# Mask pieces made between the steps of the first graph, and a last group of steps by halves of its queries, in a masked attention layer over eight graphs

## The chip, the cores and the metric

The kernel runs on one core of a Trainium2 chip. The metric is the device time of one execution in microseconds, lower being better. The kernel before takes 3193.34 us, the median of three runs (3188.96 to 3195.69).

## The reference

Eight graphs of 2048 nodes with 256 channels share one adjacency matrix of int32 zeros and ones (2048x2048), which is the attention mask. All values are f32.

```python
qkv = x @ w_qkv                                  # x: (8, 2048, 256)
q, k, v = split(qkv), each as 8 heads of 32
scores = einsum('fnhd,fmhd->fhnm', q, k) / sqrt(32)
attn = softmax(where(adj > 0, scores, -1e9))
t = einsum('fhnm,fmhd->fnhd', attn, v)           # back to (8, 2048, 256)
y = layernorm(x + t) * ln1_g + ln1_b
h = relu(y @ w1 + b1)
z = layernorm(y + h @ w2 + b2) * ln2_g + ln2_b
out = layernorm(x + z)                           # mean and variance over the 256 channels
```

## The kernel before

The work is cut into 1024 items (L543): graph `f`, chunk `qc` of 512 queries, half `g` of the heads (four heads), block `mb` of 128 keys, the last fastest. One graph is 128 steps (`FRAME`), one group (f, qc, g) is 16. Step t of the loop at L606 does, in this order on each engine's queue: `advance(t)`, which issues side work; the exponentials of item t+1 on ScalarE (ACT, L237); the scores of item t+2 on TensorE (PE, L230), each half of them followed by an addition of the mask on VectorE (DVE, L233) from PSUM into a `p` tile; the values of item t on PE (L249); and `add_up` (L264), which sums the exponentials for the softmax denominator. Of 16 items, six are added on GpSimd (POOL, L271) into the first, six go by accumulating DMAs of POOL's queue (L268) into two more chain heads. The three chain heads and item 15 are then reduced by matmuls with a constant (L315) in `denominator` (L297). Scores use three pairs of PSUM banks; two more banks alternate between the values' sums and side work, so side work has one bank a step.

The engines run in program order each, and the program writes that order out. The order of the side work is set by a small planner, `advance` (L511). Side jobs are generators in a list sorted by due step. A job yields `BANK` when it needs the side bank, `MORE` when it goes on in the bank that it has, `WAIT` when it must hold it, or a number of steps to sleep. Each step grants a credit of 2200 (`STEP`), at most 2200 (`KEPT`); a transposition of four blocks costs 1400, a unit of four matmuls of 512 columns 2048, and a job starts while 1024 are left or when it is due. Side jobs of a plain graph are the transposition of the next graph's x (`turn`: an SP load of x at L172, five steps later the transposes at L95 and copies at L166, then a write to DRAM), its queries (`ask`), its keys and values (`project`), started by the table `NEXT` (L553), and, for each query chunk, `denominator`, `outcome`, `divide` and `tail` (L297 to L377): division by the denominator (L356), first norm, feed-forward, second and third norm. A norm (L274) takes statistics on DVE (L278, L279), four small operations on POOL (L283 to L287) and scales on ACT (L290).

The mask is kept as 8-bit pieces of 128 keys x 2 blocks x 512 queries. `begin` (L557) makes all of them ahead of the loop, from 16 chunks of the adjacency matrix of 512 queries x 512 keys, in the order of query chunk: each chunk is loaded by SP (1 MB), turned to bf16 on DVE (L582), transposed on PE (L141), brought to 8 bits by ACT (L147) and DVE (L145) in turn, and written to a DRAM table `MD` (L148). After the last chunk of `qc` 1 `begin` issues the scores of items 0 and 1 and the exponential of item 0 (L598); the chunks of `qc` 2 and 3 follow, and then the loop starts. In the loop `load_mask` (L150) reads the pieces back for the next query chunk, one every other step of the groups with g = 1.

At the end, the last chunk's closing is `finish` (L443): after the last step it divides all 512 queries, and then runs two halves of 256 rows through norm, feed-forward and norms by turns (`half_rows`, L396). The chunk before it goes through `tail` with x already loaded (`xb`) and two statistics a step.

Of the kernel before, what the change touches and what calls it, by code (L numbers as in the profile page):

```python
# [10 lines left out]
F32 = mybir.dt.float32  # L11
# [50 lines left out]
def fast_path(ctx, tc, cst, x, adj, out, RS):  # L62
# [61 lines left out]
    MD = dp.tile([NCK, MB // 2, P, 2 * CH // 4], I32, name="md")  # L124
    MK = {}

# [7 lines left out]
    def mask_blocks(qc, mc, cv, to=None):  # L134
        for half in range(2):
# [12 lines left out]
            nc.sync.dma_start(MD[qc, k], words(m))  # L148

    def load_mask(f, qc, k):  # L150
        nc.sync.dma_start(words(mask_piece(f, qc, k)), MD[qc, k])
# [17 lines left out]
    def turn(f, c):  # L169
        yield INPUTS - 2  # L170
        xc, xT = take([P, TPC, C], F32), take([P, 2, CH], F32)
        nc.sync.dma_start(xc, x[f, c * CH:(c + 1) * CH, :].rearrange("(j p) c -> p j c", p=P))  # L172
        yield 5
        yield from turn_rows(xc, xT)
        give(xc)
        yield 1
        nc.sync.dma_start(XD[f][c], xT)
        XT[f, c] = xT
        give(xT)
# [38 lines left out]


    PT, O, OT, RC, DT = {}, {}, {}, {}, {}  # L220

    def scores(item):
        f, qc, g, mb = item
        pt = PT[item] = pp.tile([P, 4, CH], F32, name="p")
        ps2 = [score_pair() for _ in range(2)]

        for half in (1, 0):
            for j in range(2):
                r = D * (2 * half + j)
                nc.tensor.matmul(ps2[half][:, j, :], KT[f, mb // TPC, g][r:r + D, (mb % TPC) * P:(mb % TPC + 1) * P],  # L230
                                 QT[f, qc, g][r:r + D, :], start=True, stop=True)
        for half, ps in enumerate(ps2):
            nc.vector.tensor_tensor(pt[:, 2 * half:2 * half + 2, :], ps,  # L233
                                    MK[f, qc, mb // 2][:, mb % 2, None, :].to_broadcast([P, 2, CH]), ALU.add)

# [5 lines left out]
    def values(item):  # L241
        f, qc, g, mb = item
        grp = (f, qc, g)
        if mb == 0:
            i = state["side"]
            O[grp] = ps_x[i].tile([P, CH], F32, name=f"x{i}")
        for h in range(4):
            r = D * h
            nc.tensor.matmul(O[grp][r:r + D, :], V[f, mb // TPC, g][:, mb % TPC, r:r + D], PT[item][:, h, :],  # L249
                             start=(mb == 0), stop=(mb == LAST))  # L250
        if mb == LAST:
            OT[grp] = op.tile([P, CH], F32, name=f"oT{g}")
            nc.scalar.copy(OT[grp], O.pop(grp))
# [6 lines left out]

    ENDED = MB - 5
    SUM = 4

    def add_up(item):  # L264
        f, qc, g, mb = item
        for chain in MOVED:
            if mb in chain[1:] and not ((f, qc, g) == items[-1][:3] and mb >= ENDED):
                nc.gpsimd.dma_start(PT[f, qc, g, chain[0]], PT.pop(item), accum_op=ALU.add)  # L268
        if mb in POOLED[1:] and not ((f, qc, g) == items[-1][:3] and mb >= ENDED):
            first = PT[f, qc, g, POOLED[0]]  # L270
            nc.gpsimd.tensor_tensor(first, first, PT.pop(item), ALU.add)  # L271


    def norm(t, per=1):  # L274
# [22 lines left out]
    def denominator(f, qc, g, ready):  # L297
        grp = (f, qc, g)
        blocks = [ALONE, MOVED[0][0], POOLED[0], MOVED[1][0]]
        late = {2: ready - 1, 3: ready}  # L300
        if (f, qc, g) == items[-1][:3]:
            blocks = [POOLED[0], 11, 12, MOVED[0][0], 13, 14, MOVED[1][0], 15]
            late = {n: len(items) - k for n, k in ((2, 2), (3, 1), (4, 1), (5, 0), (6, 0), (7, 0))}
        yield BANK
# [26 lines left out]
        begin = items.index((f, qc, g, LAST)) + SUM + 2  # L331
        start(begin, outcome(f, qc) if (f, qc) != (F - 1, NCK - 1) else finish(f, qc), begin)

    def outcome(f, qc):
        yield ROOM
        state["tails"] += 1
        xin = x[f, qc * CH:(qc + 1) * CH, :].rearrange("(p j) c -> p j c", p=P)
        y = yp.tile([P, TPC, C], F32, name="y")
        yield from divide(f, qc, y)
        nc.gpsimd.dma_start(y, xin, accum_op=ALU.add)  # L340
        begin = items.index((f, qc, 1, LAST)) + SUM + 2
        if (f, qc) == (F - 1, NCK - 2):
            xb = take([P, TPC, C], F32)
            nc.sync.dma_start(xb, xin)
            start(begin + 8, tail(f, qc, y, xin, 2, xb), begin + 11)
        else:
            start(begin + 10, tail(f, qc, y, xin), begin + 26)
# [12 lines left out]
    def tail(f, qc, y, xin, per=1, xb=None):  # L360
# [5 lines left out]
        z = y  # L366
        yield from norm(z, per)
        nc.gpsimd.tensor_tensor(z, z, rows(cst["g2r"]), ALU.mult)  # L368
# [3 lines left out]
        if xb is None:  # L372
            nc.gpsimd.dma_start(z, xin, accum_op=ALU.add)
            yield 7
        yield from norm(z, per)
# [19 lines left out]

    def half_rows(h, y, xr, xb, yT, hT, dst):  # L396
        own = slice(2 * h, 2 * h + 2)
        q = slice(2 * h * P, 2 * (h + 1) * P)
        y, xr, xb = y[:, own], xr[:, own], xb[:, own]

        def row2(v):
            return v[:, None, :].to_broadcast([P, 2, C])

        nc.vector.tensor_tensor(y, y, xr, ALU.add)
        if h:
            yield
        found = half_stats(y)
        yield
        half_norm(y, *found)
        nc.gpsimd.tensor_tensor(xr, y, row2(cst["g1r"]), ALU.mult)  # L410
        nc.gpsimd.tensor_tensor(xr, xr, row2(cst["be1b2r"]), ALU.add)  # L411
        yield
        ps = bank()
        transposes(ps, [y[:, j, a * P:(a + 1) * P] for a in range(2) for j in range(2)])
        for a in range(2):
            nc.scalar.activation(yT[:, a, q], ps[:, a * 2 * P:(a + 1) * 2 * P], AF.Identity,
                                 bias=cst["be1c"][:, a:a + 1], scale=cst["g1c"][:, a:a + 1])
        yield
        ps = bank()
        for d in range(2):  # L420
            for a in range(2):
                columns(ps[:, d * 2 * P:(d + 1) * 2 * P], w1s[:, a, d * P:(d + 1) * P], yT[:, a, q], start=(a == 0), stop=(a == 1))
            nc.scalar.activation(hT[:, d, q], ps[:, d * 2 * P:(d + 1) * 2 * P], AF.Relu, bias=cst["b1s"][:, d:d + 1], scale=1.0)  # L423
        yield
        ps = bank()
        for j in range(2):
            for d in range(2):
                columns(ps[:, j * C:(j + 1) * C], hT[:, d, (2 * h + j) * P:(2 * h + j + 1) * P], w2s[:, d, :],
                        start=(d == 0), stop=(d == 1))
        z = y  # L430
        nc.vector.tensor_tensor(z, ps.rearrange("p (b c) -> p b c", c=C), xr, ALU.add)
        found = half_stats(z)
        yield
        half_norm(z, *found)
        yield
        nc.vector.tensor_tensor(z, z, row2(cst["g2r"]), ALU.mult)  # L436
        nc.vector.tensor_tensor(z, z, xb, ALU.add)  # L437
        found = half_stats(z)
        yield
        half_norm(z, *found)  # L440
        nc.sync.dma_start(dst[:, own], z)

    def finish(f, qc):  # L443
        y = yp.tile([P, TPC, C], F32, name="y")
        xr, xb = state["rows"]
        yield from divide(f, qc, y)
        yT, hT = (work.tile([P, 2, CH], F32, name=n) for n in ("turned", "hT"))
        dst = out[f, qc * CH:(qc + 1) * CH, :].rearrange("(p j) c -> p j c", p=P)
        both = [half_rows(h, y, xr, xb, yT, hT, dst) for h in range(2)]
        while both:  # L450
            for e in list(both):
                if next(e, both) is both:
                    both.remove(e)
            yield 1

# [55 lines left out]
    def advance(t, finish=False):  # L511
# [15 lines left out]
        for e in list(fill):  # L527
            while e[2] is not None and e[0] <= t and e is not state["holder"]:
                if e[2] == BANK:
                    if not free or not more():  # L530
                        break
                    free = False
                elif e[2] < INPUTS:
# [14 lines left out]
    def ask(f, c):  # L548
# [6 lines left out]
            104: [(project, 0, 1)], 108: [(project, 1, 1)], 112: [(project, 2, 1)], 116: [(project, 3, 1)]}  # L555

    def begin():  # L557
        todo = deque((qc, c) for qc in range(NCK) for c in range(NCK))
        rows, cols = [], deque()
# [43 lines left out]
    for _ in begin():  # L603
        pass
    state["side"] = 0
    for t, (f, qc, g, mb) in enumerate(items):  # L606
        if g == 1 and mb % 2 and (f + 1 < F or qc + 1 < NCK):
            load_mask(f + (qc + 1) // NCK, (qc + 1) % NCK, mb // 2)
        for what, *which in NEXT.get(t % FRAME, []):
            to = f if what is ask and which[0] else f + 1  # L610
            if to < F:
                at = (0, 0, 0) if what is turn else (which[0], 0, 0) if what is ask else (0, which[1], which[0] * TPC)
                start(t, what(to, *which), t + 3 * MB if what is turn else items.index((to, *at)) - LEAD - 1)
        if t == len(items) - MB // 2:
            xr, xb = state["rows"] = [take([P, TPC, C], F32) for _ in range(2)]
            nc.sync.dma_start(xr, x[f, qc * CH:(qc + 1) * CH, :].rearrange("(p j) c -> p j c", p=P))
        if t == len(items) - 2:
            nc.gpsimd.tensor_tensor(xb, xr, rows(cst["be2r"]), ALU.add)
# [14 lines left out]
        if mb == LAST and t + 1 < len(items):  # L633
            start(t + 2, denominator(f, qc, g, t + SUM), t + SUM + 4)
        if t == len(items) - 3:
            start(t, denominator(f, qc, g, t), t)
    t = len(items)
# [244 lines left out]
```

## Time and profile before

| | us |
|---|---|
| median of three runs | 3193.34 |
| the profiled execution | 3196.28 |
| its span, first to last instruction | 3194.5 |
| PE busy | 3081.7 |
| DVE busy | 2749.6 |
| POOL busy | 2593.3 |
| ACT busy | 2417.7 |
| mean granted clock of PE, of 1 | 0.987 |
| scores of item 0 start | 58.81 |
| scores of item 2 start | 96.55 |
| last values (L249) start | 3146.17 |

The 128 steps of a graph, counted from the starts of L230, take 400.1 us in graph 0 (with the gap between items 1 and 2), 391.7 in graph 1, and 379.4 to 381.6 in the others.

A timeline line of the profile gives start, duration, engine, line, operation, written and read tiles, shapes, and how many instructions were taken together; the bracket says how long the engine had been idle and what ended that. Ends of matmuls are modelled. A line of the stretches gives length, and busy time with the number of instructions for PE, PE's weight loads, DVE, ACT and POOL, then the granted clock, the busy share of the DMA engines, and GB/s.

### The profile page before, as it was taken

Reading aid. Unit: us, or ns where it says so; the run is one execution under the profiler, and the core shown is the slowest. Engines: PE = TensorE matmul, PEld = TensorE weight load, DVE = VectorE, ACT = ScalarE, POOL = GpSimd, SP = SyncE. Lnnn points to the kernel's source line nnn. Section 1 sums busy time; section 2 is a strip of 40 time slices with the busy share of each in tenths; the row PEclk is TensorE's granted clock in tenths of the full one; section 3 lists DMA queues with packets and bytes.
Section 4 is the critical chain, followed back from the end, with each engine's and each line's share of the span. In section 5 each row is a group of like instructions: output and inputs, shape, how many; then the busy total and the mean of one; then the engine's idle time right before and its main releaser. Section 6 shows DMA issues by size and latency. Waiting matters only on the chain. (4 is left out here: it accounts for less than half of the span.)

```text
span 3194.5 us, 68226 instructions
## 1 busy us (share of the span) xinstructions
PE 3081.7 (96%) x28868; PEld 963.0 (30%) x28868; DVE 2749.6 (86%) x3139; ACT 2417.7 (76%) x1909; POOL 2593.3 (81%) x1361
## 2 busy tenths in 40 slices
PE   7899999999999999999999999999999999999985
PEld 4222333222332223332333323323233233332222
DVE  4798988888889988889988988988988888889985
ACT  3677778777787777788777788778778778777774
POOL 0578888788888888888888888888889788889875
PEclk8899999999999999999999999999999999999998
DMA  9688889788798888898888899888879788888872
GB/s 323 142 192 193 183 175 199 161 188 189 179 195 188 191 194 178 176 204 196 187 177 174 194 208 198 168 182 196 196 174 203 177 196 192 176 177 166 178 150 64
DMA packets 153096, 589.46 MB, mean 185 GB/s; under 512 B 15024, under 2 KB 67760, under 8 KB 103888
## 3 DMA queue, kind: packets, MB, share of 16 engines
q0 software_dynamic: 64128, 433.22, 68.8%
q1 hardware_dynamic: 87840, 150.50, 13.7%
q8 instruction: 228, 3.74, 0.4%
q10 hardware_dynamic: 816, 1.31, 0.1%
q14 instruction: 84, 0.69, 0.1%
HBM read 146.67 MB, written 37.75 MB: 58 GB/s over the span
## 5 line engine op out<-in xcount | busy, mean ns | idle before, releaser
L233 DVE TENSOR_TENSOR p<-s,mask 128x1024 f32<-128x1024 f32 x2048 | 2409.1, 1218 | 325.0 <-PE s L230 182.9
L237 ACT ACTIVATE p<-p 128x2048 f32<-128x2048 f32 x1024 | 1956.0, 1910 | 566.5 <-DVE p L233 481.1
L271 POOL TENSOR_TENSOR p<-p 128x2048 f32<-128x2048 f32 x382 | 1875.4, 4909 | 359.1 <-ACT p L237 358.8
L230 PE MATMUL s<-qT,kT 32*128 32x512 f32 x8192 | 1172.5, 642 | 44.2 <-DVE p L233 39.4
L249 PE MATMUL x<-p,v 128*32 128x512 f32 x8192 | 1093.5, 606 | 4.6 <-ACT p L237 4.6
L230 PEld LDWEIGHTS s<-qT,kT 32*128 32x128 f32 x8192 | 320.9, 183 | 671.3 <-DVE p L233 643.6
L268 POOL DMA_DIRECT2D p<-p x382 | 416.8, 1092 | 70.1 <-ACT p L237 46.4
L249 PEld LDWEIGHTS x<-p,v 128*32 128x32 f32 x8192 | 161.5, 108 | 784.0 <-issue 310.2
L315 PE MATMUL x<-p,halves 128*32 128x512 f32 x2080 | 269.9, 595 | 0.0
L54 PE MATMUL x<-in,wqkv 128*32 128x512 f32 x1888 | 245.7, 592 | 0.0
L290 ACT ACTIVATE y<-y,nb,rs 128x256 f32<-128x256 f32 x372 | 219.1, 591 | 6.1 <-POOL nb L287 5.9
L278 DVE BATCH_NORM_STATS2 st<-y 128x6 f32<-128x256 f32 x372 | 155.0, 417 | 1.8 <-POOL y L370 1.8
L54 PE MATMUL x<-turned,w1s 128*32 128x512 f32 x992 | 123.9, 593 | 0.0
L54 PE MATMUL x<-w2s,hT 128*32 128x256 f32 x2016 | 121.8, 382 | 0.0
L54 PEld LDWEIGHTS x<-wqkv,in 128*32 128x32 f32 x3584 | 102.2, 110 | 64.1 <-issue 55.9
L54 PE MATMUL x<-wqkv,in 128*32 128x128 f32 x3584 | 117.4, 273 | 0.0
L315 PEld LDWEIGHTS x<-p,halves 128*32 128x32 f32 x2080 | 67.9, 111 | 156.9 <-issue 155.5
L368 POOL TENSOR_TENSOR y<-y,g2r 128x1024 f32<-128x1024 f32 x31 | 101.6, 3278 | 6.4 <-ACT y L290 6.4
L54 PEld LDWEIGHTS x<-in,wqkv 128*32 128x32 f32 x1888 | 61.3, 110 | 141.3 <-issue 116.5
L284 POOL TENSOR_TENSOR rs<-rs,mhalf 128x4 f32<-128x4 f32 x93 | 96.3, 1035 | 7.8
L370 POOL TENSOR_TENSOR y<-y,be2r 128x1024 f32<-128x1024 f32 x30 | 94.6, 3155 | 0.4
L54 PEld LDWEIGHTS x<-w2s,hT 128*32 128x32 f32 x2016 | 65.9, 111 | 70.7 <-issue 38.5
(121 smaller groups left out, 1301.1 us busy)
## 6 DMA issues: line engine op xcount, KB each, us to landing
p<-p POOLq DMA_DIRECT2D x382, 1024.0 KB, 10.0
in<-xd SPq DMA_DIRECT2D x87, 512.0 KB, 8.9
mask<-md SPq DMA_DIRECT2D x248, 128.0 KB, 8.6
y<-in_x_dram POOLq DMA_DIRECT2D x61, 512.0 KB, 10.1
p<-in_adj_dram SPq DMA_DIRECT2D x16, 1024.0 KB, 9.3
out_dram<-y SPq DMA_DIRECT2D x31, 512.0 KB, 6.2
in<-in_x_dram SPq DMA_DIRECT2D x30, 512.0 KB, 10.6
xd<-in SPq DMA_DIRECT2D x28, 512.0 KB, 8.8
```

The costliest lines, as they stand in the source:

```text
L54: nc.tensor.matmul(out[r:r + D], lhsT[:, r:r + D], rhs, start=start, stop=stop)
L230: nc.tensor.matmul(ps2[half][:, j, :], KT[f, mb // TPC, g][r:r + D, (mb % TPC) * P:(mb % TPC + 1) * P], QT[f, qc, g][r:r + D, :], start=Tr ...
L233: nc.vector.tensor_tensor(pt[:, 2 * half:2 * half + 2, :], ps, MK[f, qc, mb // 2][:, mb % 2, None, :].to_broadcast([P, 2, CH]), ALU.add)
L237: nc.scalar.activation(PT[item], PT[item], AF.Exp, scale=1.0 / math.sqrt(D))
L249: nc.tensor.matmul(O[grp][r:r + D, :], V[f, mb // TPC, g][:, mb % TPC, r:r + D], PT[item][:, h, :], start=(mb == 0), stop=(mb == LAST))
L268: nc.gpsimd.dma_start(PT[f, qc, g, chain[0]], PT.pop(item), accum_op=ALU.add)
L271: nc.gpsimd.tensor_tensor(first, first, PT.pop(item), ALU.add)
L278: nc.vector.bn_stats(st, t[:, j, :])
L284: nc.gpsimd.tensor_tensor(rs, rs, cst["mhalf"], ALU.pow)
L290: nc.scalar.activation(t[:, j, :], t[:, j, :], AF.Identity, bias=nb[:, j:j + 1], scale=rs[:, j:j + 1])
L315: nc.tensor.matmul(ps[r:r + D, :], cst["halves"][:, g, :], term[:, h, :], start=(n == 0), stop=(n == len(blocks) - 1))
L368: nc.gpsimd.tensor_tensor(z, z, rows(cst["g2r"]), ALU.mult)
```

## The change

`begin` makes the mask for `qc` 0 and 1 only. The 16 pieces of `qc` 2 and 3 are made by `mask_job`, side jobs of the first graph's steps: one is started every third step from step 2. Each uses two spare tiles of 256 KB (five pairs at most, taken from buffers that the first graph needs later), loads its part of the adjacency matrix in rows of 128 numbers, sleeps five steps, casts to bf16 on ACT, transposes on PE, and brings the result to 8 bits on DVE. `load_mask` waits in the program until its piece has been issued. The projections of graph 0's side work move a few steps back (`LATER`).

`turn` sleeps seven steps instead of five after its load, but for graph 1. The last group takes two key blocks and 256 queries a step, the first half of the queries in its steps 0 to 7; `closing(h)` then is a side job for each half, which takes the place of `finish`. In the last graph, the tails of the chunks before it start earlier or with fewer pauses, and x is loaded earlier.

```diff
+    def mask_job(n):
+        while not spare:
+            yield 1
+        parts, until = spare.popleft()
+        qc, k = divmod(n + MB, MB // 2)
+        for b, part in enumerate(parts):
+            nc.sync.dma_start(part.bitcast(I32).rearrange("p (j m) -> p j m", j=TPC),
+                              adj[qc * CH:(qc + 1) * CH, (2 * k + b) * P:(2 * k + b + 1) * P].rearrange("(j p) m -> p j m", p=P))
+        yield 5
+        cv = [part.bitcast(BF16)[:, 0:CH] for part in parts]
+        for b, part in enumerate(parts):
+            nc.scalar.copy(cv[b], part.bitcast(I32))
+            yield 1
+        yield BANK
+        ps = bank(BF16)
+        state["credit"] -= TURN
+        for b in range(2):
+            for j in range(TPC):
+                nc.tensor.transpose(ps[:, b, j * P:(j + 1) * P], cv[b][:, j * P:(j + 1) * P], identb)
+        m = parts[0][:, CH // 2:CH].bitcast(F8).rearrange("p (b q) -> p b q", b=2)
+        nc.vector.tensor_scalar(m.bitcast(I8), ps, 0.0, CODE, op0=ALU.is_le, op1=ALU.mult)
+        yield 1
+        nc.sync.dma_start(MD[qc, k], words(m))
+        MADE.add((qc, k))
+        yield 3
...
-        yield 5
+        yield 5 if f == 1 else 7
         yield from turn_rows(xc, xT)
...
+    def closing(h):
+        f, qc, g = ENDING
+        own, part, t0 = slice(2 * h, 2 * h + 2), slice(h * HQ, (h + 1) * HQ), len(items) - MB // 2 * (2 - h)
+        terms = [(5, 6), (1, 7), (0, 7), (6, 8), (7, 8)]
...
+        for n, (block, when) in enumerate(terms):
+            if n:
+                yield MORE
+            while state["now"] < t0 + when:
+                yield WAIT
...
+        if h:
+            rc, den = turned_sums()
...
-        yield from norm(z, per)
+        yield from norm(z, per if per == 1 else TPC)
...
-                    free = False
+                    free = state["side"] is None
...
-        todo = deque((qc, c) for qc in range(NCK) for c in range(NCK))
+        todo = deque((qc, c) for qc in range(2) for c in range(NCK))
...
+            while ((qc + 1) % NCK, mb // 2) not in MADE:
+                advance(t0, finish=True)
+                t0 += 1
...
+        while n_mask < MB and t >= 2 + 3 * n_mask:
+            start(t, mask_job(n_mask), 3 * MB - 2 + 2 * n_mask if n_mask < MB // 2 else 4 * MB - 2 + 2 * n_mask)
+            n_mask += 1
...
-        if t == len(items) - 3:
-            start(t, denominator(f, qc, g, t), t)
+        for h in range(2):
+            if t == len(items) - MB // 2 * (2 - h) + 4:
+                start(t + 1, closing(h), len(items) - h)
```

## The prediction, made before the changed kernel was run

> **What bounds the kernel now.** I read the busy shares first, then the busy time by stretches, then the timeline of the opening, of plain steps and of the end, and last the DMA issues.
>
> ```profile
> PE 3081.7 (96%) x28868; PEld 963.0 (30%) x28868; DVE 2749.6 (86%) x3139; ACT 2417.7 (76%) x1909; POOL 2593.3 (81%) x1361
> ```
>
> TensorE (PE) leads, but 96% is a mean. The stretches (busy us of PE, PEld, DVE, ACT, POOL, then clock, DMA share, GB/s) show an opening in which nothing is full:
>
> ```profile
> 60.00:80.00 20.00, 9.64 (x72) 7.01 (x72) 13.27 (x16) 5.88 (x5) 0.00 (x0) 0.53 0.82 289
> 80.00:100.00 20.00, 11.01 (x80) 7.22 (x80) 12.15 (x15) 5.93 (x6) 0.00 (x0) 0.50 0.29 88
> 3150.00:3195.00 45.00, 15.35 (x152) 7.57 (x152) 17.18 (x58) 12.33 (x24) 17.13 (x22) 0.69 0.07 25
> ```
>
> The PE timeline there: the scores of items 0 and 1 at 58.81 and 61.35, then eight mask chunks (transposes L141, each waiting for DVE's L582), and scores of item 2 only at 96.55.
>
> ```profile
> 61.35 2.09 PE L230 MATMUL s<-qT,kT 32*128 32x512 f32 x8 [1.40 <-DVE p L233]
> 66.52 1.03 PE L141 MATMUL s<-identb,p 128*128 128x128 bf16 x8 [3.08 <-DVE p L582]
> ...
> 93.34 1.89 PE L141 MATMUL s<-identb,p 128*128 128x128 bf16 x16 [1.98 <-DVE p L582]
> 96.55 2.09 PE L230 MATMUL s<-qT,kT 32*128 32x512 f32 x8 [1.32 <-DVE in L145]
> ```
>
> Later steps come in kinds, read as distances between starts of L230. With one unit of side work (four L54 matmuls of 512 columns) a step is 2.92 us and PE never idles. With four transposes (L95) it is 2.65 to 2.74; with two units 3.78. A bare step is 2.55 and PE waits 0.41 for DVE, whose two mask additions (L233) take 2.36:
>
> ```profile
> 119.80 1.14 PE L230 MATMUL s<-qT,kT 32*128 32x512 f32 x8
> ...
> 122.73 1.14 PE L230 MATMUL s<-qT,kT 32*128 32x512 f32 x8
> ...
> 130.85 1.14 PE L230 MATMUL s<-qT,kT 32*128 32x512 f32 x8 [0.41 <-DVE p L233]
> 133.40 1.14 PE L230 MATMUL s<-qT,kT 32*128 32x512 f32 x8 [0.41 <-DVE p L233]
> ```
>
> So a step is PE-bound with side work and DVE-bound without. Two other holes matter: x loads that land late (PE, second graph), and the last groups:
>
> ```profile
> 610.76 1.03 PE L95 MATMUL x<-ident,in 128*128 128x128 f32 x4 [4.06 <-DMA in<-in_x_dram]
> ```
>
> ```profile
> 3091.86 5.43 POOL L271 TENSOR_TENSOR p<-p 128x2048 f32<-128x2048 f32 x1
> ...
> 3099.29 1.09 ACT L290 ACTIVATE y<-y,nb,rs 128x256 f32<-128x256 f32 x2 [5.60 <-POOL nb L287]
> ```
>
> There POOL's norm stands behind a 5.43 us addition, ACT stands behind the norm, and PE behind the exponential.
>
> **What the Trainium skill says.** "VectorE: DVE Perf Modes", section "Why PSUM operands drop a tier": a PSUM operand caps an operation at 2×_1P; section "What auto-detection actually checks": that mode wants every tensor 16-bit. The new mask operation reads bf16 in PSUM and writes 8 bits, so it runs at one element a cycle. The cycle table under that page's "The TRN2 errata" gives (120 + 1024)/0.96 = 1.19 us; the trace has 1.22 for L145, which reads and writes the same types. "TensorE: Matmul & The Clock Gate", "Part 1: The HAM clock gate": the array runs at half clock until busy for about 3.4 us. The trace agrees: clock 0.53 and 0.50 above, and L230 at 2.09 against 1.14. "DMA: Bandwidth & Descriptors", "Queues, rings and completion order": each DMA engine goes round its queues packet by packet, so small packets share time with large ones. No run here has shown 512-byte rows in such company.
>
> **The change, part by part.**
>
> *Opening.* The chunks of query chunks 2 and 3 go. Scores of item 2 need the first PSUM pair of item 1, which DVE frees 1.18 into its L233 at 63.51, so at about 64.7. Removed: 96.55 − 64.7 = 31.8 us. The slow-clock ramp after it (L230 starts at 96.55, 100.43, 103.84, 106.33) stays and moves forward.
>
> *Sixteen mask pieces in steps 2 to about 85.* Each adds two SP loads of 256 KB, two ACT casts (128x512, priced as L166: 0.58), eight bf16 transposes (0.46 to 1.03 by L141), one DVE operation (1.22) and one SP write. In the changed program's order they fall on steps that were 11 bare, 4 with a unit and 1 with two: 11 × 2.54 + 4 × 2.92 + 3.78 = 43.4 us before. Now DVE sets them. Below: bare steps at 3081.00, 3084.33 and 3087.69 which hold two L278/L279 pairs (1.08 us more DVE) took 3.33 and 3.36. Above: 2.54 + 1.22 = 3.76. I take 3.4: 16 × 3.4 − 43.4 = +11.0 (+9.4 to +16.8). The units displaced double up later: six more doubled steps in graphs 1 and 2 (12 to 16 and 12 to 14), 6 × 0.855 = +5.1 (+2.6 to +6). ACT: an exponential and a cast are 1.91 + 0.58 = 2.49 in 2.55, hidden if nothing else is there; where a copy joins it pushes the exponential, +1.5 (0 to +3).
>
> *Late loads.* A cast waits in ACT's order for its load, with all exponentials behind it and PE behind those. It has five steps, 5 × 2.92 = 14.6 us. Nothing of before shows it; the nearest rows are these:
>
> ```profile
> p<-p POOLq DMA_DIRECT2D x382, 1024.0 KB, 10.0
> in<-in_x_dram SPq DMA_DIRECT2D x30, 512.0 KB, 10.6
> ```
>
> In 560 to 660 the x loads needed 19.9 against the same lead and stalled twice, 12.5 us of step time together with their slow clock: 6.25 each. The added demand is 16 × 1024 packets. By bytes of queue q1 (13.7% of 16 × 3194.5 for 150.5 MB) they cost 24 us of all engines, by its mean packet (80 ns) 82 us, in some 240 us where the DMA share is 0.83. That makes 0.93 to 1.17: from nearly full to over-full. What else is queued slips with it: on SP the x loads, the mask reads (L151) and the reloads of x, on POOL's queue the additions of L268, whose sum PE reads (L315) four steps after the group's last item, some 11 us against a landing of 10.0. I take one stall of that size, +6 (0 to +28, between four and five). A gain is excluded: before, no step of this stretch waited for such a load. The mask reads that now wait for a piece to be made (pieces of chunk 2 finished by step 33, first read at step 49) cost nothing.
>
> *yield 7.* x loads of graphs 2 onward get two more steps (5.8 us), over the stalls of 4.06 and 3.49: −10 (−12.5 to 0: nothing if other transfers delay the load by as much again).
>
> *The last two groups.* The step at 3094.59 lasts 7.64 to 3102.23, −6.5 at most; bare steps with statistics gain 2.5; but four statistics (0.54 from start to start) and four L290 (1.08 a pair) now fall together, 1.1 more on DVE or ACT than two, in three norms or so, and the chunk's work is squeezed into fewer steps: 3 to 5 back. −4 (−8 to +2). The last group's steps by two blocks and 256 queries have the same elements on DVE and ACT; on PE sixteen matmuls of 256 columns took 1.04 (L54 at 3174.53) where eight of 512 take 1.06, so nothing.
>
> *Closing chain.* After the last L249 at 3146.17 come 44.1 us to the end of the last L394. After it, 2 denominator terms instead of 3, −0.86. Before, DVE was held from 3151.77 to 3155.95 by the other chunk's statistics, and the second half went last; the first half now goes through under the steps. Against that, the second half's nb still waits on DVE and ACT where the halves interleave: −3 (−6 to +1). The rows x for the end are loaded 16 steps ahead on SP and one POOL addition moves with them: no price, since DMA there is at 0.47 between 3100 and 3150.
>
> Sum: −31.8 + 11.0 + 5.1 + 1.5 + 6 − 10 − 4 − 3 = **−25.2**. The profiled execution took 3196.28 (span 3194.5 and 1.8 around it), giving 3171.1; it lies 2.9 above the median 3193.34, so on the median's footing **3168**.
>
> **Rivals.**
> A. *DVE is the bound and nothing is won elsewhere.* Mask steps 3.76 (+16.8), graph 1 stalls unchanged, casts +3, the end −4: −31.8 + 16.8 + 5.1 + 3 + 6 − 4 = −5, **3188**. For: bare steps wait on DVE. Against: statistics of similar length cost 0.8 only.
> B. *Everything is hidden.* +9.4, +2.6, no cast and no load stall, −12.5, −8, −6: −46, **3147**. Against: DMA share 0.83 and PE full with side work.
> C. *Casts wait for loads (slower).* Place: ACT, steps 8 to 83. Price 6.25 a stall, the half of 12.5 above. Without the +6 the sum is −31.2, so five stalls (31.3) eat all, and from six or seven on the kernel is slower by over 0.2%. Half of the pieces, eight stalls, give −31.2 + 50 = +19, **3212**. For: the five-step lead is the one that failed twice in graph 1, and packets are small. Against: the first pieces' loads start before the POOL queue fills, and the median landing was 10.6.
>
> **Numbers.** Forecast 0.62 (own range 3158 to 3179), A 0.16, B 0.12, C 0.10. The range leaves out C and most of B: 3153 to 3190. This measurement can tell about 0.2% (6.4 us) from no change: faster takes the forecast, B and a third of A (0.79), same most of A (0.10), slower C (0.11).
>
> **What would show it.** Item 2's scores near 65 us and clock 1.0 by 80; steps with eight bf16 transposes at 3.3 to 3.5 and DVE named ahead of L230; graph 0, start to start of L230 over 128 steps, at about 387 us (400.1 before); no PE wait on x loads in graph 1, which takes about 385 (391.7 before); ACT idle before a cast, released by a load, under 10 us in sum; last L249 to last ACT 41 us. I am wrong if casts wait over 30 us, if mask steps exceed 3.8, or if the first graph is not shorter than 395.

## The result, and the profile after

The changed kernel takes 3170.38 us (median of six runs, 3167.9 to 3170.59) beside 3195.05 of the kernel before on the same chip: ratio 0.9923, 95% interval 0.9913 to 0.9934, which is 24.7 us less. Forecast were 25.2. The profiled execution has a span of 3168.7 us, 25.8 below that of before. The sum held; several of its terms did not, and that their errors cancelled is luck. The rest of this text is about which.

The busy line of the page and the stretches of the opening (same columns as before: PE, PEld, DVE, ACT, POOL, clock, DMA share, GB/s):

```profile
PE 3075.1 (97%) x29220; PEld 970.7 (31%) x29220; DVE 2752.2 (87%) x3138; ACT 2424.2 (77%) x1934; POOL 2592.1 (82%) x1358
```

```profile
60.00:80.00 20.00, 15.99 (x92) 3.63 (x96) 14.53 (x14) 9.90 (x6) 3.39 (x1) 0.74 0.63 171
80.00:100.00 20.00, 19.65 (x164) 5.20 (x156) 17.22 (x15) 17.46 (x15) 17.81 (x8) 1.00 0.91 184
```

Between 80 and 100 us PE is busy for 19.65 of 20 us at full clock where it was busy for 11.01 at half clock. The PE timeline of the opening shows the hole gone: item 2's scores (L276 here) start 3.44 us after item 1's, not 35.20 (61.35 to 96.55 before).

```profile
62.70 2.09 PE L276 MATMUL s<-qT,kT 32*128 32x512 f32 x8 [1.40 <-DVE p L279]
66.14 2.09 PE L276 MATMUL s<-qT,kT 32*128 32x512 f32 x8 [1.34 <-DVE p L279]
```

The mask pieces run in the steps. This is the timeline of PE and DVE around pieces 0 and 1. A step, counted from scores to scores, with only a piece's transposes (L168) stays near 2.6; the step after it, in which DVE does the 1.21 us operation (L170), is 3.33 and 3.39, and the next scores wait for DVE:

```profile
95.33 1.14 PE L276 MATMUL s<-qT,kT 32*128 32x512 f32 x8
97.40 0.40 PE L168 MATMUL x<-identb,kT 128*128 128x128 bf16 x4
97.95 1.14 PE L276 MATMUL s<-qT,kT 32*128 32x512 f32 x8
98.88 1.21 DVE L170 TENSOR_SCALAR kT<-x 128x1024 int8<-128x1024 bf16 x1
101.28 1.14 PE L276 MATMUL s<-qT,kT 32*128 32x512 f32 x8 [0.53 <-DVE p L279]
102.28 1.21 DVE L170 TENSOR_SCALAR turned<-x 128x1024 int8<-128x1024 bf16 x1
104.67 1.14 PE L276 MATMUL s<-qT,kT 32*128 32x512 f32 x8 [0.47 <-DVE p L279]
```

Of the 16 steps that hold an L170, 13 take 3.26 to 3.40. Two that hold a unit of side work too take 4.04 and 3.96, and one takes 5.73 for the reason that follows.

A late load did stop ACT, as feared, but in two places only: 2.44 us here and 1.86 at 168.46. The next exponential (L283) and the copy that ends the group (L314) stand behind the cast, PE's values stand behind the copy, and the step takes 5.73 us instead of 2.93:

```profile
158.64 1.14 PE L276 MATMUL s<-qT,kT 32*128 32x512 f32 x8
159.56 0.62 ACT L161 CAST kT<-kT 128x512 bf16<-128x512 int32 x1 [2.44 <-DMA kT<-in_adj_dram]
...
161.90 0.57 ACT L314 COPY oT<-x 128x512 f32<-128x512 f32 x1
162.52 1.06 PE L310 MATMUL x<-p,v 128*32 128x512 f32 x8 [2.74 <-ACT oT L314]
...
164.37 1.14 PE L276 MATMUL s<-qT,kT 32*128 32x512 f32 x8
```

And something that the forecast did not have: in the last graph one DVE addition of 128x1024 numbers took 5.00 us. It starts 0.6 us after the start of a POOL addition and ends 1.1 us after that one's end, and PE's next scores wait 5.05:

```profile
3050.39 4.51 POOL L339 TENSOR_TENSOR p<-p 128x2048 f32<-128x2048 f32 x1 [0.29 <-ACT p L283]
3050.99 5.00 DVE L411 TENSOR_TENSOR y<-y,in 128x1024 f32<-128x1024 f32 x1
...
3057.17 2.09 PE L276 MATMUL s<-qT,kT 32*128 32x512 f32 x8 [5.05 <-DVE p L279]
```

After the last values (L298, 3127.99) the last norm's ACT instructions now end 36.1 us later (3163.04 + 1.09), where it was 44.1:

```profile
3127.99 1.05 PE L298 MATMUL x<-p,v 128*32 128x256 f32 x16
...
3133.56 0.76 DVE L522 TENSOR_TENSOR y<-s,rc 128x256 f32<-128x256 f32 x2
...
3139.48 1.09 ACT L467 ACTIVATE y<-y,nb,rs 128x256 f32<-128x256 f32 x2 [10.01 <-DVE nb L465]
...
3163.04 1.09 ACT L467 ACTIVATE y<-y,nb,rs 128x256 f32<-128x256 f32 x2 [0.20 <-DVE nb L465]
```

Here is the whole difference of the spans, read from the starts of the score matmuls (a graph is 128 steps from item 1 of it on; graph 7 ends at the last scores), for before, after, and the runs below. Each row is one profiled execution.

| kernel | item 0 starts | graph 0 | graph 1 | graph 2 | graphs 3 to 6 | graph 7 | from the last scores to the end | span |
|---|---|---|---|---|---|---|---|---|
| before | 58.8 | 400.1 | 391.7 | 379.4 | 1524.9 | 381.6 | 55.4 | 3194.5 |
| after | 60.2 | 381.1 | 383.4 | 381.4 | 1525.6 | 386.8 | 47.6 | 3168.7 |
| mask_only | 58.1 | 380.0 | 383.4 | 381.4 | 1525.2 | 382.2 | 55.3 | 3168.2 |
| yield7_only | 60.1 | 400.7 | 378.8 | 381.2 | 1525.5 | 381.6 | 55.3 | 3185.9 |
| later_only | 61.4 | 398.6 | 381.6 | 381.3 | 1525.0 | 381.5 | 55.3 | 3187.2 |
| ending_only | 58.0 | 398.4 | 388.3 | 379.4 | 1526.8 | 387.2 | 47.3 | 3187.9 |
| after_yield5 | 58.4 | 381.7 | 383.4 | 381.4 | 1525.2 | 386.2 | 47.9 | 3166.8 |
| no_pieces | 60.2 | 366.9 | 381.2 | 381.2 | 1525.5 | 386.9 | 46.9 | 3151.5 |
| dve_twice | 59.4 | 402.3 | 383.5 | 381.2 | 1525.6 | 386.5 | 46.8 | 3187.8 |
| loads_twice | 59.1 | 416.4 | 383.1 | 381.4 | 1525.5 | 386.5 | 47.3 | 3201.8 |
| lead7 | 59.8 | 397.1 | 382.0 | 381.9 | 1525.0 | 386.8 | 47.3 | 3182.5 |
| psum_add | 59.8 | 381.1 | 383.4 | 381.4 | 1525.2 | 382.8 | 47.8 | 3164.1 |
| pool_free | 60.5 | 381.5 | 383.4 | 381.4 | 1525.2 | 383.3 | 47.8 | 3165.7 |
| both_mends | 61.6 | 377.8 | 383.4 | 381.4 | 1525.7 | 382.9 | 47.8 | 3163.2 |

A row's columns add up to its span but for some 2.5 us, the distance from item 0 to item 1. Item 0 starts between 58.0 and 61.6. Before, yield7_only and later_only have the same opening and start it at 58.8, 60.1 and 61.4, so some 3 us between two spans need not be the edit's; what makes this difference was not looked into. A stretch with a late load varies as much: ending_only, whose steps of graph 1 are those of before, takes 388.3 there and not 391.7.

### The profile page after: what moved, and what is told of

The parts are those of the page before. It is cut to its first block, busy times and chain, and to the rows that moved or that the text cites. A ratio compares the mean times of both kernels' runs of the same rounds, so it can differ in the third digit from the quotient of the medians.

```text
span 3168.7 us, 68994 instructions
## 1 busy us (share of the span) xinstructions
PE 3075.1 (97%) x29220; PEld 970.7 (31%) x29220; DVE 2752.2 (87%) x3138; ACT 2424.2 (77%) x1934; POOL 2592.1 (82%) x1358
## 3 DMA queue, kind: packets, MB, share of 16 engines
q1 hardware_dynamic: 100640, 150.50, 14.1%
## 4 chain that ended last, share of the span: by engine, by line
## 5 line engine op out<-in xcount | busy, mean ns | idle before, releaser
L279 DVE TENSOR_TENSOR p<-s,mask 128x1024 f32<-128x1024 f32 x2016 | 2371.5, 1218 | 305.9 <-PE s L276 173.4
L283 ACT ACTIVATE p<-p 128x2048 f32<-128x2048 f32 x1024 | 1955.8, 1910 | 568.4 <-DVE p L279 465.5
L339 POOL TENSOR_TENSOR p<-p 128x2048 f32<-128x2048 f32 x378 | 1846.0, 4884 | 336.7 <-ACT p L283 336.3
L276 PE MATMUL s<-qT,kT 32*128 32x512 f32 x8064 | 1154.7, 642 | 48.4 <-DVE p L279 44.5
L310 PE MATMUL x<-p,v 128*32 128x512 f32 x8064 | 1076.5, 606 | 3.5 <-ACT oT L314 3.5
L276 PEld LDWEIGHTS s<-qT,kT 32*128 32x128 f32 x8064 | 315.9, 183 | 655.6 <-DVE p L279 628.6
L336 POOL DMA_DIRECT2D p<-p x378 | 407.5, 1079 | 69.5 <-ACT p L283 41.4
L382 PE MATMUL x<-p,halves 128*32 128x512 f32 x2016 | 261.1, 592 | 0.3 <-ACT turned L575 0.3
L54 PE MATMUL x<-in,wqkv 128*32 128x512 f32 x1888 | 245.6, 592 | 1.5 <-DVE y L170 0.8
L54 PE MATMUL x<-turned,w1s 128*32 128x512 f32 (+1 forms) x1024 | 126.9, 593 | 0.3 <-ACT in L194 0.3
L54 PEld LDWEIGHTS x<-wqkv,in 128*32 128x32 f32 x3584 | 102.2, 110 | 62.9 <-issue 54.5
L54 PE MATMUL x<-w2s,hT 128*32 128x256 f32 x2016 | 120.3, 379 | 0.0
L54 PE MATMUL x<-wqkv,in 128*32 128x128 f32 x3584 | 117.1, 273 | 0.0
L54 PEld LDWEIGHTS x<-in,wqkv 128*32 128x32 f32 x1888 | 61.1, 110 | 143.4 <-issue 114.8
L54 PEld LDWEIGHTS x<-w2s,hT 128*32 128x32 f32 x2016 | 65.5, 110 | 68.9 <-issue 35.6
```

The costliest lines, as they stand in the source:

```text
L54: nc.tensor.matmul(out[r:r + D], lhsT[:, r:r + D], rhs, start=start, stop=stop)
L283: nc.scalar.activation(PT[item], PT[item], AF.Exp, scale=1.0 / math.sqrt(D))
L382: nc.tensor.matmul(ps[r:r + D, :], cst["halves"][:, g, :], term[:, h, :], start=(n == 0), stop=(n == len(blocks) - 1))
```

## Experiments: which part of the change did what

**mask_only.** The kernel before with `mask_job`, `begin` for two query chunks and `LATER`; sleeps of five steps and the old end.

```diff
+    def mask_job(n):
...
-        todo = deque((qc, c) for qc in range(NCK) for c in range(NCK))
+        todo = deque((qc, c) for qc in range(2) for c in range(NCK))
...
-        for what, *which in NEXT.get(t % FRAME, []):
+        for what, *which in (NEXT if f else {**NEXT, **LATER}).get(t % FRAME, []):
```

> The kernel before with only the mask pieces moved into the first graph's steps (and the projections of that graph moved with them); five steps of sleep for every x load and the old end stay. Theory: the hole between items 1 and 2 goes (-31.8), the rest of graph 0 gains 12.8 of it back as in the changed kernel, the units pushed over cost some 5 in graphs 1 and 2, and the two late x loads of graph 1 stay: about 3195 - 14 = 3181. Rival, that the late loads of graph 1 went because the first graph's work was shifted and not because of the longer sleep: -14 - 12 = about 3169.

Measured: 3171.68 (3169.36 to 3173.47) against 3191.93; ratio 0.9934 (0.9921 to 0.9946). The rival was right: graph 1 takes 383.4 as in the changed kernel, without the longer sleep. This part alone gives nearly the whole gain (ratio 0.9923 with all parts).

**yield7_only.** `yield 5` in `turn` becomes `yield 5 if f == 1 else 7`; nothing else.

> The kernel before with only the longer sleep after the x loads of graphs 2 to 7. Theory: graph 1 loses its two waits for x loads and their slow clock, -10 to -12: about 3184. Rival (the loads just stall later, or the shift of the first graph did it): no change, 3195.

Measured: 3186.48 (3183.08 to 3187.81); ratio 0.9981 (0.9972 to 0.9990). Graph 1 loses 12.9, graphs 0 and 2 give 2.5 back. Alone, the longer sleep removes the two stalls; the total gains less, 5.5 by the medians and 8.6 by the spans. But it does not do it by the 5.8 us of two more steps. From the load to its transposes there were 14.8 us before (load issued at 591.94, transposes ready at 606.70, which is 610.76 less their wait of 4.06). Here there are 29.2 (SP's queue and PE):

```profile
593.89 0.39 SPq L172 DMA_DIRECT2D in<-in_x_dram  x1
```

```profile
611.27 1.04 PE L315 MATMUL x<-p,halves 128*32 128x512 f32 x8
...
623.08 0.66 PE L95 MATMUL x<-ident,in 128*128 128x128 f32 x4
```

In between stand the four units of the group's sums (L315), each with the one side bank of its step. Before, the transposes came first and the sums after them:

```profile
591.94 0.39 SPq L172 DMA_DIRECT2D in<-in_x_dram  x1
```

```profile
614.89 1.03 PE L315 MATMUL x<-p,halves 128*32 128x512 f32 x8
```

**after_yield5.** The changed kernel, with `yield 5` for every graph.

> The changed kernel with five steps of sleep for every x load. Theory: the two waits of graph 1 come back, +8 to +12 over the changed kernel's 3170: 3178 to 3182. Rival, that the shift alone cured them: 3170.

Measured: 3168.58 (3167.04 to 3170.43); ratio 0.9925 (0.9912 to 0.9938), the same as the changed kernel. Together with the first two runs: in the changed kernel the longer sleep is worth nothing. The gain of graph 1 has another cause. The timelines of PE and of SP's queue in this run show how the late loads were avoided: the load issued at 580.62 is transposed at 606.93, 26.3 us later instead of 14.8.

```profile
606.93 0.66 PE L95 MATMUL x<-ident,in 128*128 128x128 f32 x4
```

```profile
580.62 1.24 SPq L200 DMA_DIRECT2D in<-in_x_dram  x1
```

**later_only.** So what put the transposes back? The suspect was the table `LATER`, which hands some projections of graph 0 to graph 1, where they are due earlier than the x transposes. The kernel before, with the table alone:

```diff
+    LATER = {80: [], 100: [(project, 2, 0)], 104: [(project, 3, 0)], 108: [(project, 0, 1)], 112: [(project, 1, 1)],
+             116: [(project, 2, 1)], 120: [(project, 3, 1)]}
...
-        for what, *which in NEXT.get(t % FRAME, []):
+        for what, *which in (NEXT if f else {**NEXT, **LATER}).get(t % FRAME, []):
```

> The kernel before with only the table of the first graph's projections moved back by a few steps (LATER); no mask pieces, five steps of sleep. Theory, that units pushed from graph 0 into graph 1 put other work ahead of the x transposes there, so that these come some 26 us after their load instead of 15 and find it landed: graph 1 falls from 391.7 to about 382, the time by 5 to 10, 3183 to 3188. Rival, that the pieces themselves shift the loads against the POOL queue: the two waits stay and the time is 3192.

Measured: 3188.0 (3185.88 to 3190.89) against 3193.53; ratio 0.9984 (0.9978 to 0.9991). Graph 1 falls from 391.7 to 381.6, and a load issued at 598.75 is transposed at 625.07, again 26.3 us:

```profile
598.75 1.25 SPq L172 DMA_DIRECT2D in<-in_x_dram  x1
```

```profile
613.26 1.04 PE L315 MATMUL x<-p,halves 128*32 128x512 f32 x8
...
625.07 0.66 PE L95 MATMUL x<-ident,in 128*128 128x128 f32 x4
```

The table alone cures graph 1. The suspect was half right: four projection units stand between load and transposes here as before; what is new is that the job comes so late in its group that the four units of the sums go first, as in yield7_only. Units moved out of graph 0 (−1.5 there, all of it in 16 steps from item 82 on) come back in graph 2 (+1.9). Whether the pieces without the table would have kept the stalls was not run.

**ending_only.** The changed kernel with all 16 chunks made ahead, the old table and sleeps of five steps.

> The changed kernel's end alone: all 16 chunks are made ahead as before and every sleep is five steps. Theory: the steps of the last graph lose 5.2, 4 of them in one long addition on DVE, and what follows the last scores gains 7.8: -2.6, about 3192. Rival, that the end is worth what was forecast in each of its parts (-4 and -3): 3188; rival, that the last graph's loss comes from the moved start of the first graph: -8, 3187.

Measured: 3191.66 (3186.14 to 3200.33); ratio 0.9996 (0.9985 to 1.0008). No change that can be measured: the interval goes from 4.8 faster to 2.6 slower. In the trace graph 7 gives 5.6 back (387.2), and what follows its last scores gains 8.1 (47.3), which leaves 2.5.

## Experiments: the long addition

**psum_add.** The quotient is written back to its PSUM bank, and x is added from there.

```diff
-            nc.vector.tensor_tensor(y, y, xb, ALU.add)
...
+            if plus is not None:
+                nc.vector.tensor_tensor(y[:, :, gg * P:(gg + 1) * P], to, plus[:, :, gg * P:(gg + 1) * P], ALU.add)
```

> The changed kernel, with the addition of x in the last graph's third chunk taken apart: the quotient is written back to its PSUM bank and x is added from there, 128x512 twice, instead of one addition of two SBUF operands (128x1024). Theory: that addition took 5.00 us because it shared a port with the POOL addition beside it; with one operand in PSUM it takes 0.68 twice and the step of 7.18 us falls to about 3.3: -4, about 3166. Rival, that the DVE waited for something else (the loaded x, or POOL's queue): the wait moves to the new additions and the time stays at 3170.

Measured: 3166.19 (3162.54 to 3167.75) against 3192.45; ratio 0.9909 (0.9893 to 0.9924); graph 7 falls by 4.0 against the changed kernel. On the timeline one of the new additions runs wholly beside a POOL addition and takes 0.69:

```profile
3043.44 4.55 POOL L339 TENSOR_TENSOR p<-p 128x2048 f32<-128x2048 f32 x1 [1.90 <-ACT p L283]
...
3044.75 0.69 DVE L431 TENSOR_TENSOR y<-x,in 128x512 f32<-128x512 f32 x1
```

**pool_free.** The DVE addition stays; the POOL addition beside it becomes an accumulating DMA.

```diff
+        if item == (F - 1, NCK - 1, 0, 8):
+            nc.gpsimd.dma_start(PT[f, qc, g, MOVED[0][0]], PT.pop(item), accum_op=ALU.add)
+            return
```

> The changed kernel, with the POOL addition of item 8 in the last chunk's first group (the one beside the long DVE addition) made by an accumulating DMA into another chain instead; the DVE addition stays as it is. Theory of the shared port: the DVE addition falls from 5.00 to about 1.2 and the time by about 4 to 3166. Rival, that 128x1024 from two SBUF operands costs 5 us by itself: it stays at 5.00 and the time at 3170.

Measured: 3166.26 (3163.21 to 3167.43); ratio 0.9908 (0.9892 to 0.9923). On the DVE timeline the same instruction (L414 here) takes 1.21:

```profile
3050.74 1.21 DVE L414 TENSOR_TENSOR y<-y,in 128x1024 f32<-128x1024 f32 x1
```

Graph 7 falls by 3.5. The intervals of both ratios overlap that of the changed kernel, so the gain is read from graph 7 and not from the medians.

Both runs say the same: this addition is slow only with two SBUF operands and only beside a POOL addition. (psum_add halves its size too; pool_free, at full size, excludes the size as the cause.) The Trainium skill has it, in "SBUF — State Buffer", section "SBUF: two separate sides": DVE with two SBUF inputs and a GpSimd operation that reads SBUF share one port pair under "an exclusive lock, not a bandwidth split", held for the whole instruction. The trace agrees: 5.00 is close to the rest of the 4.51 us POOL addition, which had 3.9 us to go, and the 1.21 of the addition itself, 5.1 together.

## Experiments: the price of the pieces

**no_pieces.** No mask job; `load_mask` reads `MD[qc % 2, k]`, so the kernel leaves out the mask of query chunks 2 and 3 and its results are not the layer's.

> The changed kernel without any of the 16 pieces' work: query chunks 2 and 3 use the mask of chunks 0 and 1, so that part of the computation is left out. It measures the price of the pieces. Theory: 12 to 13 in graph 0, of which casts that came late are 4, and some 2 for displaced units: about 3157. Rival A (pieces bound by DVE at 3.76 a step, the rest of the first graph faster for another reason): 3150. Rival, pieces nearly free: 3166.

Measured: 3151.68 (3149.69 to 3153.25); ratio 0.9863 (0.9848 to 0.9878). The spans differ by 17.2 from the changed kernel, 14.1 of it in graph 0 and 2.4 in graphs 1 and 2.

**dve_twice.** L170 is issued twice for each piece.

> The changed kernel with the DVE operation of each mask piece (L170, 1.21 us) done twice. Theory, that DVE sets the steps that follow a piece's transposes: eleven or so of the 16 fall on steps without a unit and cost 1.2 each in full, the others less: +13 to +19 over 3170, 3183 to 3189. Rival, that the price of a piece is on PE or ACT: +0 to +6.

Measured: 3190.89 (3187.95 to 3193.12) against 3193.53; ratio 0.9990 (0.9981 to 0.9999), so nearly the whole gain of the change is gone. Graph 0 grows by 21.2, 1.3 a piece: the step after a piece's transposes grows by 1.25 to 1.27 in 14 of 16 cases, also in one that holds a unit (the other with a unit grows by 2.04, and one was the late step of 5.73). So DVE sets these steps, and not PE or ACT. The timeline of PE and DVE has the next piece's transposes waiting for DVE:

```profile
95.81 2.48 DVE L171 TENSOR_SCALAR kT<-x 128x1024 int8<-128x1024 bf16 x2
98.43 0.61 PE L168 MATMUL x<-identb,turned 128*128 128x128 bf16 x8 [1.42 <-DVE kT L171]
99.47 1.14 PE L277 MATMUL s<-qT,kT 32*128 32x512 f32 x8 [0.43 <-DVE p L280]
```

**loads_twice.** Each piece's two adjacency loads are issued twice.

> The changed kernel with each mask piece's two adjacency loads issued twice. If the rows of 512 bytes fill the DMA engines (rival C of the prediction, near its edge), casts wait for late loads in many pieces and x loads of the first graph too: +15 to +40 over 3170. If there is room, ACT's waits for loads stay at the two of 2.44 and 1.86, and the time within 5 of 3170.

Measured: 3205.71 (3200.9 to 3210.36); ratio 1.0036 (1.0022 to 1.0049): slower than before. Graph 0 takes 35.3 more than in the changed kernel. Five steps of 9.1 to 11.3 us hold it; the waits of ACT for late loads are

```profile
ACT kT L162 <- DMA kT<-in_adj_dram: 12.4, 2, 6.3
ACT turned L162 <- DMA turned<-in_adj_dram: 9.4, 1, 9.4
ACT y L162 <- DMA y<-in_adj_dram: 6.6, 1, 6.6
```

(total, times, longest), and PE waits 6.0 for one x load. Two issues of the same load also stand longer in SP's queue, so this run doesn't separate the DMA engines from the queue.

**lead7.** Seven steps between a piece's loads and its first cast.

> The changed kernel with seven steps between the adjacency loads of a mask piece and its first cast, five before. Theory: the two waits of ACT for a late load (2.44 and 1.86) go, and with them the 2.8 of the 5.73 us step and about 1 more: -3 to -4, about 3167. Rival, that the spare buffers then come back later and the pieces bunch up near their due time: no gain or a loss of a few us, 3170 to 3174.

Measured: 3184.48 (3182.53 to 3185.9); ratio 0.9970 (0.9959 to 0.9981), 14 us slower than the changed kernel. The rival's mechanism came true, at a larger size. ACT's waits shrink to one of 1.0. But a piece keeps its spare buffers two steps longer, the last two are not made when `load_mask` asks for them, and the planner then issues the side work that it has with no step between. On PE's timeline scores come at 332.88 and next at 352.90, with L54 and L95 units and the transposes of a piece between them; a step of 10.41 for the last piece follows:

```profile
332.88 1.14 PE L276 MATMUL s<-qT,kT 32*128 32x512 f32 x8
...
352.90 1.14 PE L276 MATMUL s<-qT,kT 32*128 32x512 f32 x8
```

**both_mends.** The changed kernel with the addition from PSUM and a longer sleep only for the two pieces whose loads were late.

```diff
-        yield 5
+        yield 7 if n in (8, 9) else 5
         cv = [part.bitcast(BF16)[:, 0:CH] for part in parts]
```

> The changed kernel with the addition taken from PSUM (as in the run psum_add) and seven steps of sleep for the two pieces alone whose casts came before their loads (numbers 8 and 9), five for the others. Theory: -4 and -3, about 3163, and graph 0 at about 378. Rival, that the wait for a late load then moves to the next pieces or that the last pieces are forced as in the run lead7: 3166 or more.

Measured: 3164.16 (3161.57 to 3174.28) against 3193.53; ratio 0.9915 (0.9895 to 0.9935). In the trace graph 0 falls by 3.2 to 377.8 and ACT no longer waits for an adjacency load; graph 7 falls by 3.9. By the ratios it cannot be told from psum_add nor from the changed kernel, whose intervals overlap with its own; the gain is read from the trace. The last two pieces are made in time.

## Why the prediction was right, point by point

- *Opening, −31.8:* 35.20 became 3.44, so −31.76. Right.
- *Mask pieces, +11.0:* without the late loads (both_mends) graph 0 is 377.8, without pieces 366.9: +10.9, casts included. Right in size and in cause: the DVE operation priced at 1.22 takes 1.21 to 1.23, and dve_twice shows that DVE sets these steps. One detail was off: the cost falls on the step after the transposes, since DVE comes to the piece one step later. The two steps with a unit (4.04 and 3.96) lie above the 3.8 that was named as a sign of being wrong; the 3.76 behind that sign was counted on a bare step. In these two DVE's operation shows as 1.0 to 1.1 over the 2.92 of a step with a unit: the unit itself waits for it (at 208.70 and 321.70 PE waits 0.77 and 0.69 for L170).
- *Doubled units, +5.1:* the trace has the six more doubled steps, 16 and 14 in graphs 1 and 2. Four of them come from the table (14 and 14 in later_only) and two from the pieces. But the units of the table were taken out of graph 0 (−1.5), which the sum left out.
- *Casts, +1.5, and late loads, +6:* the two late loads cost 3.2 (381.1 to 377.8); the casts' crowding cannot be seen apart. Over-sized by some 4. The mechanism of rival C is real: double the loads and it costs 35 us. Of the two counts of the added traffic, the one by bytes fits: the DMA share is 0.93 between 84 and 330 us.
- *yield 7, −10:* this step was wrong, and its number right by luck. Graph 1 did lose 8.3, and with the doubled units added back about 10; but the longer sleep has no part in it (after_yield5). The prediction counted the distance from load to transposes as the steps of the sleep, and did not ask what else stands ahead of the transposes for the one side bank. There it is the sums: behind them the distance is 26.3 us (after_yield5, later_only) and not 14.8. The trace of the changed kernel alone would have confirmed the wrong reason.
- *The last two groups, −4, and the closing chain, −3:* −7 together. From item 1 of graph 7 to the end the changed kernel gains 2.6. What failed is the term for the last two groups: it left out the DVE addition of x (L411) that takes the place of an accumulating DMA. By its length alone that is 1.21 us of DVE; behind POOL's lock it was 5.00. With it mended (psum_add) the gain is 6.5, close to the 7.
- *How the two divide* is less sure than the table makes it look: graph 7 went from 381.6 to 386.8 and the rest from 55.4 to 47.6, but the border between them, the last scores, moved against the work. Four units of the last group's sums (L490, 4.1 us of PE) now stand ahead of the last scores; before, all of that group's stood behind. The old stall is gone. It was read as 7.64 between two starts of values (L249); from scores to scores, as the other steps are counted, it was 10.19 (3096.45 to 3106.64). Against that, the four statistics in one step cost more than was priced: the step at 3013.21 takes 4.41 and the next 3.71, 3.0 more than two bare steps.
- *The reason given for the closing chain,* that the first half goes through under the steps, holds only for its sums. Its division (L522) starts at 3133.56, after the last values, 3.1 ahead of the second half's at 3136.66. After the last values the first norm's ACT instruction comes at 11.5 us, 14.7 before, and from there to the end it is 24.7 instead of 29.4. The two halves now follow each other more closely (3.0 us between their first ACT instructions, 5.1 before); which of the new orders makes it is not shown by a run of its own.

So the sum came out because errors cancelled: +4.4 at the end, −5.7 in graph 0, −1.4 in graphs 1 and 2, and +2.1 in what no term was about (the start of item 0, and graphs 3 to 6). Rivals A and B fell: the mask steps were 3.26 to 3.40 and not 3.76, and not free. Rival C fell by the count, two stalls where five would have eaten the gain.

## What to carry to other kernels

Work moved out of a prologue into a loop costs what the engine that is late in those steps pays for it: here DVE, 1.21 us a piece of which 0.7 to 0.85 shows in a step without a unit, and not the engine with the highest busy share. When a stall disappears after a change of several parts, run the parts alone and the whole without each: here the part that was meant to cure the stall could, but another had already done so, and both by the same way round, a place in the queue for the side bank. A lead time between a load and its use is paid for with buffers held longer; lengthen it where the trace shows a wait and not everywhere.

## What the hardware showed unexpectedly

A DVE addition of two SBUF operands took 5.00 us instead of 1.21 when a POOL addition was under way, and 0.69 for half the size beside one when an operand was in PSUM. Doubling 16 pairs of loads of 256 KB in rows of 512 bytes, 8 MB more in some 250 us, turned a kernel 0.8% faster than before into one 0.4% slower; how much of that is the DMA engines and how much the longer queue of SP stays open.
